# Attention probabilities brought to keys on partitions: 32x32 blocks transposed by VectorE and a trip through DRAM, in place of TensorE transposes and copies

## The chip, the cores and the metric

One core of one Trainium2 chip runs the whole kernel. The metric is the device time of one execution in microseconds (us). Before the change the median of three runs is 2646.62 us (2646.61 to 2647.22).

## The reference, cut to what matters

The input has 8 sequences of 512 tokens with 256 features. Each goes through four transformer layers (two layers, a recurrence with a learned matrix, then the same two layers again). The change lies in the local attention of these layers: 8 heads of 64, windows of 128 tokens; a query sees its own window and the one before, at most 128 keys back.

```
def _layer(x, wqkv, qs, ksc, wo, lg, lb, w1, b1, w2, b2):
    qkv = shift_token(x) @ wqkv                       # 256 -> 3 * 512
    q, k, v = heads of qkv;  q, k = rotary_xpos(l2norm(q) * qs, l2norm(k) * ksc)
    sim = einsum('bhwid,bhwjd->bhwij', 8 * q, k of this window and the one before)
    sim = where(mask, -max, sim)                      # mask: i < j, i > j + 128, no key
    attn = softmax(sim, axis=-1)
    out = einsum('bhwij,bhwjd->bhwid', attn, v)
    x = x + out @ wo
    ... layer norm, 256 -> 2 * 682, gated by gelu, 682 -> 256, added to x
```

All arithmetic is in float32.

## The kernel before, in words

**Work.** `sequence(b)` describes one sequence as a graph of nodes: two halves of two layers each, `attention` and `feed_forward`, with `ttt`, the recurrence, between the halves. An attention handles its four windows of 128 tokens one after another: transpose of x (`h.turn`), projections (`qk`, line 717, and `v`, line 804), rotation and norms, transposes of q and k (`qk.turn`, line 828). Then, twice per window, a group `g` of four heads:

- `sc` (line 868): TensorE computes scores. Its tile is used in quarters of 64 x 64, so that blocks that the window never reaches are left out. Queries lie on partitions, keys along the free dimension. From the second window on a query has 192 key columns (`nj`), in the first 128.
- `least` (line 911, DVE) adds the mask and finds the extreme of a row, `exp` (line 923, ACT) exponentiates and sums, one instruction per head; `recip` (line 936 DVE or 938 POOL) and `shares` (line 944, DVE or POOL) scale by the sum, one instruction of each for two heads.
- `pr.turn` (line 970): TensorE transposes the probabilities, 16 matmuls with the identity per group (8 in the first window), because the next product needs keys on partitions. `pr.copy` (line 629, in the helper `copy`, ACT or DVE) copies the two PSUM banks to `prT`.
- `po` (line 1007): TensorE multiplies values by the transposed probabilities, again in quarters; `po.copy` and `po.add` put the result together, and `py` (line 1058) projects it with `wo`. `x.attn` (line 1067) adds it to x.

There are 8 x 4 x 4 x 2 = 256 such groups. In the feed-forward, `hs.shift` (lines 1085, 1086, 1088) shifts x by one token with SBUF-to-SBUF DMAs; the matmuls are at lines 1151, 1242 and 1255.

**Order.** Nothing is ordered by hand. `Scheduler.run` goes through the graph like a planner: each node has an engine (or a choice of two), a cost in ns, buffers that it takes, and a `tail`, the ns until its result can be read. At each step the node that can start first goes next, corrected by `EARLY`, a table of ns per node name, and by `varied`, a pseudo-random correction by stretches of 5 us that the list `VARIED` steers. The instructions are then issued in that order on every engine, and each engine works through its own list in order. Up to three sequences are under way at a time (the pool `lane`). TensorE's nodes have a kind (`full`, `rows`, `quad`: the whole array, halves, quarters), and a change of kind has a planned cost.

**Queues.** All DMAs are issued by SyncE (SP), on one queue: loads of weights and x at the start, `hs.shift`, reloads of x (line 1760), and stores of the result (line 1790).

**Buffers** that the change touches: `pr` 6 of 128 x 512, two per group, with zeros at both edges of each row (written at line 1801), so that a transpose can read past the 192 columns; `prT` 2 of 128 x 1024; `s8` 8 for the sums; 8 PSUM banks, of which a group takes two for its transposes.

Of the kernel before, what the change touches and what calls it, by code (L numbers as in the profile page):

```python
# [12 lines left out]
ALU = mybir.AluOpType  # L13
# [12 lines left out]
GATE = 64  # L26
NH1 = 2 * NFC * P + GATE + REM
# [87 lines left out]
def t_pool(n, spread=False):  # L115
# [6 lines left out]
    "XT6": 200,  # L122
    "_full_quad": 850,
    "_full_rows": 350,
    "_quad_full": 400,
    "_quad_rows": 450,
    "_rows_full": 500,
    "_rows_quad": 650,
    "_table": -250,
    "base.x": -700,  # L130
    "base.y": 50,
    "base.z": -550,
    "below": -250,
    "block": 1000,
    "bx": 500,
    "bx.copy": -450,
    "bx6": 1000,
    "bx6.copy": -1000,
    "cross.mask": 2000,
    "down": -300,  # L140
# [4 lines left out]
    "gram": -50,  # L145
    "gram.copy": -750,
    "h.copy": -1650,
    "h.edge": 2100,
# [4 lines left out]
    "hs.rstd": -1350,  # L153
    "hs.stats": 100,
    "hs.zero": -400,
    "k.scale": 2350,
    "keys": -200,
    "keys.copy": -300,
    "kq": 5100,
    "kq.copy": -1000,  # L160
    "last": 200,
    "last.gelu": -650,
    "least": -250,
    "norm 0": 100,
    "norm 1": 400,
    "ones": 2100,
    "po": 3300,
    "po.add": 50,
    "po.copy": 100,
    "pr.copy": -250,  # L170
    "pr.turn": 150,
# [3 lines left out]
    "qk.add": -100,  # L175
    "qk.copy": 100,
# [3 lines left out]
    "qk.swapped": 2800,  # L180
    "qk.turn": 5050,
    "recip": 950,
    "remains": 650,
    "rest": -200,
    "rope": -2950,
    "sc": 2350,
    "sequence 4": 350,
    "shares": -50,
    "start": 1000,
    "tv": 2350,  # L190
    "u": 5500,
    "u.copy": -100,
    "v": -50,
    "value": 150,
    "w": 4650,
    "w.add": 350,
    "x.ffn": 200,
    "x.rstd": -1900,
    "x.scale": -500,
    "x.stats": 500,  # L200
    "xbx": 2650,
    "xbx.t": 500,
    "xbx6": 1000,
    "y": 300,
    "z.rstd": -400,
    "z.scale": 50,
    "z.stats": 5600,
    "zT": -450,
    "zero": -1000,
    "zn.rstd": -1850,  # L210
    "zn.scale": -350,
    "zn.stats": -500,
    "zn.turn": 4500,
# [6 lines left out]
    11539, 59206, 52431, 7169, 51312, 47193, 35081, 54701, 2496, 7793, 6049, 56177, 10364, 34536,  # L220
    8294, 4310, 20154, 19168, 52227, 29170, 16540, 21667, 50441, 20648, 28762, 21176, 51225, 49241,
    45956, 34971, 21009, 28142, 19477, 38168, 5557, 12352, 7023, 53196, 6017, 32604, 32616, 33833,
    43497, 35592, 8, 9511, 36946, 21011, 40384, 28542, 18616, 35469, 46717, 3648, 49052, 34713,
    26816, 29204, 8404, 4647, 15343, 36844, 570, 21424, 12355, 42492, 50428, 45178, 54350, 17920,
    13395, 135, 39989, 44533, 2549, 22957, 29261, 17027, 29544, 14357, 27402, 53285, 13020, 11910,
    26247, 40152, 22117, 30422, 46544, 22999, 49636, 47593, 30197, 3179, 35589, 32132, 42056, 18356,
    57054, 3385, 45135, 14935, 20770, 32612, 13353, 15733, 35692, 48376, 37702, 12678, 33060, 54960,
    27803, 54969, 53369, 31335, 34476, 36715, 13, 17472, 3933, 49344, 40320, 43761, 51808, 53819,
    30473, 58888, 28378, 53574, 53586, 34808, 30271, 11754, 5097, 46663, 4587, 12477, 2842, 20974,
    22949, 16164, 56345, 59752, 37818, 42810, 36514, 28003, 38920, 15614, 32190, 14889, 45329,  # L230
    56333, 3909, 22135, 44005, 49596, 54630, 11534, 50699, 55304, 13694, 14380, 32785, 48251, 51975,
    59596, 39815, 34672, 26684, 43342, 49501, 38504, 13035, 9055, 59153, 49831, 29616, 8451, 2950,
    5921, 10921, 22426, 31491, 10417, 40901, 35295, 21598, 37874, 47623, 56332, 58977, 50639, 51395,
    14345, 21523, 1611, 59581, 38356, 9024, 8797, 9600, 33490, 20077, 18908, 39770, 12624, 0, 51302,
    12996, 28627, 14230, 30261, 45539, 33994, 58844, 55888, 53070, 40769, 41472, 42381, 21824,
    25505, 26825, 37644, 26704, 31501, 49830, 52837, 21763, 24330, 27631, 47626, 31160, 32421,
    20990, 43125, 47451, 26149, 56263, 41669, 38285, 29128, 53275, 59120, 363, 15861, 23553, 38689,
    16, 59208, 8741, 59992, 24971, 2133, 29045, 13059, 56697, 49647, 42350, 46546, 32101, 980,
    58623, 42263, 42129, 58230, 58436, 55171, 53628, 11325, 17446, 17234, 26564, 12471, 44487,
    47246, 47905, 19512, 6228, 20309, 9884, 23474, 21539, 12749, 53397, 58236, 36711, 21477, 28615,  # L240
    11585, 23822, 4616, 960, 14012, 19245, 52408, 9606, 51939, 36194, 40143, 58969, 31327, 21363,
    19023, 20707, 24836, 4653, 46695, 9517, 40252, 20970, 35385, 8326, 20484, 11202, 51312, 9682,
    42952, 35195, 31373, 29093, 31724, 58081, 5082, 52637, 24194, 57630, 47639, 14785, 25712, 17698,
    27876, 35732, 43008, 43338, 18992, 8751, 5850, 25733, 15460, 31028, 26546, 27345, 36488, 44056,
    33295, 58977, 39749, 29184, 25121, 23756, 33811, 26536, 2260, 15160, 321, 39968, 25191, 31222,
    45604, 48604, 7672, 56893, 14684, 26720, 30312, 41919, 57072, 2421, 44875, 34765, 3604, 10279,
    45490, 35361, 22716, 21175, 46557, 5008, 49647, 1355, 7859, 39941, 43761, 4026, 49030, 9539,
    56965, 8358, 3988, 59899, 58021, 13265, 53954, 9411, 13889, 26300, 5547, 22515, 925, 22821,
    35389, 36309, 3233, 50482, 32683, 44192, 45433, 54698, 24152, 37273, 3714, 29516, 35158, 19134,
    31173, 30908, 46863, 51249, 42973, 41570, 7558, 58198, 43105, 36002, 53169, 27713, 15508, 57450,  # L250
    13353, 45327, 20959, 21312, 25608, 23768, 55045, 27334, 58634, 20168, 34664, 55665, 6316, 39132,
    11849, 10070, 18798, 46877, 11811, 49462, 58565, 1501, 28373, 7960, 55865, 56429, 52621, 1403,
    19983, 51522, 6552, 248, 6935, 6388, 4871, 4789, 20877, 23567, 24542, 21112, 42445, 40535,
    41468, 43567, 1697, 53106, 45256, 50440, 21162, 41824, 59524, 4758, 53095, 48105, 39745, 19805,
    15895, 4145, 51961, 47869, 41251, 39860, 1162, 32717, 5615, 59674, 43307, 49529, 2408, 1126,
    6903, 26424, 10998, 1128, 11983, 31727, 294, 20411, 37533, 25779, 45123, 39019, 22071, 17092,
    35693, 44717, 33182, 15800, 26669, 36844, 32178, 27395, 16355,
# [189 lines left out]
def macaron_kernel(ctx: ExitStack, tc: tile.TileContext, a: dict, out: bass.AP):  # L447
# [4 lines left out]
    ps = ctx.enter_context(tc.tile_pool(name="ps", bufs=1, space=bass.MemoryType.PSUM))  # L452
    engines = {"ACT": nc.scalar, "DVE": nc.vector, "POOL": nc.gpsimd}
# [15 lines left out]
    def both_of(*vals):  # L469
# [3 lines left out]

    pools = {
# [9 lines left out]
        "pr": buffers("pr", 6, [P, 8 * DH]),  # L484
        "prT": buffers("prT", 2, [P, 4, 4, DH]),
# [9 lines left out]
        "s8": buffers("s8", 8, [P, 8]),  # L495
# [23 lines left out]
    def load_x(b, w=None):  # L519

        if not w:
            lane[b], first_x[b] = Val("lane"), Val("x")
        own = slice(0, NW) if w is None else slice(w, w + 1)
        if w == 0 and b >= 2:
            taken[b] = node("lane.take", (b, -NW - 1), "SP", 0.0, lambda e: None, takes=[lane[b], first_x[b]], tail=0.0)
        order[0] += 1
        n = node(
            "load.x",
            (-1, order[0]) if b < 2 else (b, (w or 0) - NW),
            "SP",  # L530
            1500.0 if w is None else 450.0,
            lambda e: dma(first_x[b].ap[:, own, :], a["x"][b].rearrange("(w p) d -> p w d", p=P)[:, own, :]),
            [taken[b]] if b in taken else [],
            takes=[] if w or b in taken else [lane[b], first_x[b]],
            uses=[first_x[b]] if w or b in taken else [],
            tail=3600.0 if w is None else 2900.0,
        )
        L["x", b] = [n] * NW if w is None else [*L.get(("x", b), []), n]
# [8 lines left out]
    def load_layer(l):  # L547
# [38 lines left out]
        W[l] = (wqkv, rt, wo, lnp, w1, b1, w2)  # L586

# [18 lines left out]
    def sequence(b):  # L606
# [62 lines left out]
        def attention(x, l, ready):  # L669
# [3 lines left out]
            n_qk = n_v = n_k = None  # L673
            for w in range(NW):
# [6 lines left out]
                    [ready[w], L["ident"]],  # L681
# [3 lines left out]
                )  # L685
                n_h = copy(
# [174 lines left out]
                for g in range(2):  # L861

                    sc, prT = [Val("ps"), Val("ps")], Val("prT")
                    prs, sts = [Val("pr"), Val("pr")], [Val("s8"), Val("s8")]

                    def scores(sc=sc, g=g, w=w, qT=qT):
# [30 lines left out]
                        takes=[*sc, *prs, *sts],  # L897
# [3 lines left out]
                    n_w = []  # L901
                    for par in range(2):

                        st = sts[par]
                        pr = lambda k, n, par=par, prs=prs: prs[par].ap[:, DH + k * 3 * DH : DH + k * 3 * DH + n]
                        exps = []
                        for k in range(2):

# [33 lines left out]
                        def shares(e, st=st, par=par, prs=prs, nj=nj):  # L942
# [13 lines left out]
                                uses=[prs[par], st],  # L956
                                port=BOTH,
                            )
                        )


                    pts = [Val("ps"), Val("ps")]
# [909 lines left out]
```

## Time and profile before

| | |
|---|---|
| time, median of 3 runs | 2646.62 us |
| span of the profiled execution | 2645.8 us |
| granted TensorE clock, mean | 1.000 |
| busy: PE / DVE / ACT / POOL | 99% / 74% / 62% / 54% of the span |
| DMA | 44.69 MB moved, mean 17 GB/s |

The span runs from the first to the last instruction of one execution; the time has 0.8 us around it. PE is TensorE's matmuls, PEld its weight loads, which run beside matmuls; DVE is VectorE, ACT ScalarE, POOL GpSimd, SP SyncE. L970 is line 970 of the kernel. A group's line gives its busy time, the mean of one instruction in ns, and the idle time of the engine just before it with what ended that idle time.

### The profile page before, as it was taken

Reading aid. Unit: us, or ns where it says so; the run is one execution under the profiler, and the core shown is the slowest. Engines: PE = TensorE matmul, PEld = TensorE weight load, DVE = VectorE, ACT = ScalarE, POOL = GpSimd, SP = SyncE. Lnnn points to the kernel's source line nnn. Section 1 sums busy time; section 2 is a strip of 40 time slices with the busy share of each in tenths; the row PEclk is TensorE's granted clock in tenths of the full one; section 3 lists DMA queues with packets and bytes.
Section 4 is the critical chain, followed back from the end, with each engine's and each line's share of the span. In section 5 each row is a group of like instructions: output and inputs, shape, how many; then the busy total and the mean of one; then the engine's idle time right before and its main releaser. Section 6 shows DMA issues by size and latency. Waiting matters only on the chain.

```text
span 2645.8 us, 77025 instructions
## 1 busy us (share of the span) xinstructions
PE 2610.2 (99%) x30608; PEld 1961.5 (74%) x30608; DVE 1968.5 (74%) x5827; ACT 1647.9 (62%) x4328; POOL 1434.5 (54%) x2045
## 2 busy tenths in 40 slices
PE   8999999999999999999999999999999999999998
PEld 5777777677777777777777777777777777776776
DVE  7776776867878767877877678787677867867755
ACT  4666667655667756665566666667557665555754
POOL 8655464546565455654644466375445754546533
PEclk9999999999999999999999999999999999999999
DMA  5000000000100000000000001000001000000000
GB/s 186 10 8 10 17 8 16 6 8 8 34 7 10 9 11 28 8 10 7 19 23 9 8 10 30 6 10 9 7 8 32 11 8 10 22 7 6 14 9 17
DMA packets 59231, 44.69 MB, mean 17 GB/s; under 512 B 8140, under 2 KB 56440, under 8 KB 58872
## 3 DMA queue, kind: packets, MB, share of 16 engines
q1 hardware_dynamic: 58872, 39.77, 5.0%
q8 instruction: 241, 3.95, 0.6%
q14 instruction: 118, 0.97, 0.1%
HBM read 18.79 MB, written 4.19 MB: 9 GB/s over the span
## 4 chain that ended last, share of the span: by engine, by line
PE 66%; DVE 3%; ACT 2%; POOL 1%; issue 1%; DMA 0%; SPq 0%; DVEq 0%; ACTq 0%; POOLq 0%
PE ps L1151 16%; PE ps L717 12%; PE ps L1242 7%; PE ps L804 6%; PE ps L1058 6%; PE ps L1007 4%; PE ps L868 4%; PE ps L970 3%; PE ps L665 2%; PE ps L828 2%; PE ps L1255 1%; PE ps L1387 1%; PE ps L1498 1%; PE ps L1483 1%; ACT pr L923 0%
## 5 line engine op out<-in xcount | busy, mean ns | idle before, releaser
L1151 PE MATMUL ps<-h2T,w 128*128 128x256 f32 (+1 forms) x2816 | 651.5, 381 | 3.2 <-ACT h2T L1129 1.4
L1151 PEld LDWEIGHTS ps<-h2T,w 128*128 128x128 f32 (+1 forms) x2816 | 518.6, 188 | 121.9 <-issue 29.4
L717 PE MATMUL ps<-wqkv,hT 128*128 128x512 f32 x1024 | 487.5, 601 | 1.9 <-DMA wqkv<-in_wqkv_dram 1.8
L923 ACT ACTIVATE pr<-pr,s 128x192 f32<-128x192 f32 (+1 forms) x1024 | 439.8, 432 | 64.5 <-DVE s L911 61.2
L753 POOL TENSOR_TENSOR st<-st,powc 128x8 f32<-128x8 f32 x256 | 439.6, 1717 | 21.3
L911 DVE CUSTOM_DVE_ANT_0 pr<-ps,amask,st 128x192 f32<-128x192 f32 (+1 forms) x1024 | 353.8, 395 | 31.1 <-PE ps L868 28.1
L944 POOL TENSOR_TENSOR pr<-pr,s 128x384 f32<-128x384 f32 (+1 forms) x313 | 243.1, 787 | 202.4 <-DVE s L936 188.3
L717 PEld LDWEIGHTS ps<-wqkv,hT 128*128 128x128 f32 x1024 | 185.5, 191 | 160.1 <-issue 140.6
L1192 DVE SCALAR_TENSOR_TENSOR gT<-ps,b,gl 128x256 f32<-128x256 f32 x320 | 152.0, 482 | 195.5 <-PE ps L1151 167.1
L1242 PE MATMUL ps<-w,gT 128*128 128x256 f32 x1280 | 291.4, 380 | 0.0
L1242 PEld LDWEIGHTS ps<-w,gT 128*128 128x128 f32 x1280 | 241.5, 190 | 48.6 <-issue 16.3
L736 ACT ACTIVATE tmp<-ps 128x512 f32<-128x512 f32 x256 | 152.1, 596 | 195.8 <-DVE rot L761 134.6
L938 POOL TENSOR_TENSOR s<-s,powc 128x2 f32<-128x2 f32 x174 | 122.8, 707 | 278.7 <-ACT pr L923 276.1
L629 ACT COPY prT<-ps 128x512 f32<-128x512 f32 (+1 forms) x322 | 157.8, 542 | 151.1 <-PE ps L970 148.4
L1058 PE MATMUL ps<-wo,oT 128*128 128x256 f32 x1024 | 243.4, 380 | 0.5 <-DVE s L911 0.3
L804 PE MATMUL ps<-wqkv,hT 128*128 128x512 f32 x512 | 240.6, 594 | 0.1
L761 DVE TENSOR_TENSOR rot<-ps,rt 128x512 f32<-128x512 f32 x256 | 175.1, 686 | 74.4 <-PE ps L717 65.3
L1058 PEld LDWEIGHTS ps<-wo,oT 128*128 128x128 f32 x1024 | 191.2, 190 | 46.9 <-issue 16.1
L1173 ACT ACTIVATE gl<-ps,b 128x256 f32<-128x256 f32 x320 | 142.9, 474 | 108.4 <-PE ps L1151 100.2
L1007 PE MATMUL ps<-prT,v 64*64 64x128 f32 (+1 forms) x7168 | 198.1, 247 | 3.3 <-DVE prT L629 2.1
L868 PE MATMUL ps<-kT,qT 64*64 64x128 f32 (+1 forms) x7168 | 193.1, 250 | 4.2 <-issue 2.1
L923 ACT ACTIVATION_READ_ACCUMULATOR pr<-pr,s 128x1 f32 x1024 | 193.7, 189 | 0.0
(124 smaller groups left out, 4420.7 us busy)
## 6 DMA issues: line engine op xcount, KB each, us to landing
hs<-x SPq DMA_DIRECT2D x128, 64.0 KB
hs<-x SPq DMA_DIRECT2D x128, 63.5 KB
base<-in_x_dram SPq DMA_DIRECT2D x8, 512.0 KB
out_dram<-base SPq DMA_DIRECT2D x32, 128.0 KB
w<-in_w_dram SPq DMA_DIRECT2D x6, 640.0 KB
x<-in_x_dram SPq DMA_DIRECT2D x28, 128.0 KB
wqkv<-in_wqkv_dram SPq DMA_DIRECT2D x2, 1024.0 KB
hs<-x SPq DMA_DIRECT2D x96, 0.5 KB
```

Source lines behind the costliest of these rows:

```text
L717: nc.tensor.matmul(pp.ap, hT[w].ap[:, c * P : (c + 1) * P], wqkv[:, c, i * INNER : (i + 1) * INNER], start=(c == 0), stop=(c == 1),)
L753: nc.gpsimd.tensor_tensor(ss, ss, powc[:, 0:HEADS], ALU.pow)
L761: nc.vector.tensor_tensor(heads(rot.ap), heads(pp.ap), tab, ALU.mult)
L804: nc.tensor.matmul(pv.ap, hT[w].ap[:, c * P : (c + 1) * P], wqkv[:, c, 2 * INNER : 3 * INNER], start=(c == 0), stop=(c == 1),)
L868: nc.tensor.matmul(sc[par].ap[half(c), k * 4 * DH + at : k * 4 * DH + at + keys.stop - keys.start], qT.ap[half(par), 2 * g + k, half(c)], ...
L911: nc.vector.tensor_tensor_reduce(out=pr(k, nj), in0=sc.ap[:, k * 4 * DH : k * 4 * DH + nj], in1=amask[:, 0:nj] if w else amask[:, 3 * DH : ...
L923: nc.scalar.activation(pr(k, nj), pr(k, nj), AF.Exp, bias=st.ap[:, k : k + 1], scale=-1.0, accum_out=st.ap[:, 2 + k : 3 + k],)
L944: (nc.vector if e == "DVE" else nc.gpsimd).tensor_tensor(both, both, st.ap[:, 4:6].unsqueeze(2).to_broadcast([P, 2, nj]), ALU.mult)
L1007: nc.tensor.matmul(po[r].ap[half(par), k * P + first : k * P + first + cols * DH], v[j].ap[half(r), hd * DH : (hd + 1) * DH], prT.ap[half( ...
L1058: nc.tensor.matmul(py.ap[:, 0:D], oT.ap[:, c, :], wo[:, c, :], start=(c == 0), stop=(c == INNER // P - 1))
L1151: nc.tensor.matmul(dst.ap[0:rows, 0 : 2 * P], w1[:, kc, col : col + rows], h2T.ap[:, kc, :], start=(kc == 0), stop=(kc == 1),)
L1242: nc.tensor.matmul(py.ap[:, 0:D], gT.ap[:, at : at + P], w2[:, c, :], start=(c == 0), stop=False)
```

## The change: what it does

For a group's four heads the probabilities now lie in one buffer `pr` of 128 x 4 x 192, with one `recip` for four heads. In place of `pr.turn` and `pr.copy` stand three nodes:

- `pr.flip`: one DVE instruction transposes each 32 x 32 block of `pr` where it stands (24 blocks of 32 columns per row of blocks, 16 in the first window) into `flip`, with the four heads side by side.
- `pr.out`: four DMAs, one for each 32 queries, write `flip` to a DRAM tile `image` with keys as rows, in runs of 512 bytes. Queries 64 to 127 are written 64 rows lower, since their keys start 64 later.
- `pr.in`: one DMA reads 128 or 256 rows of the image back to `prT`, keys on partitions, 2048 bytes per row.

The parts of the image that nothing writes are set to zero once (`load_zeros`, two DMAs at the start, ahead of the second load of x). `weigh` (`po`) reads `prT` by its new layout; its matmuls are as many and as large as before. Buffers: `pr` 4, `flip` 3, `image` 6, `prT` 3, `s8` 5 with 16 columns. The DMA descriptor scratch is set to 1024. `h.turn` of a window now comes after that of the window before, and a sequence's lane is taken in order. The tables `EARLY` and `VARIED` have new values throughout, so the whole order of work is another one.

```
+    images = dram.tile([6, 2 * P, P // BLK, 4 * BLK], F32, name="images")
-        "pr": buffers("pr", 6, [P, 8 * DH]),
-        "prT": buffers("prT", 2, [P, 4, 4, DH]),
+        "pr": buffers("pr", 4, [P, 4, 3 * DH]),
+        "flip": buffers("flip", 3, [P, 3 * DH // BLK, 4, BLK]),
+        "image": [images[n] for n in range(images.shape[0])],
+        "prT": buffers("prT", 3, [P, 2, P // BLK, 4, BLK]),
...
+    def load_zeros():
+        flat = pools["flip"][0][0:DH].rearrange("p m h i -> p (m h i)")[:, 0 : 8 * BLK]
+        n = node("zeros", (-1, 0), "POOL", 400.0, lambda e: nc.gpsimd.memset(flat, 0.0))
+        def emit(e):
+            for lo, q in ((0, 2), (3 * DH, 0)):
+                dst = images[:, lo : lo + DH, q : q + 2, :].rearrange("n p q e -> p n (q e)")
+                dma(dst, flat.unsqueeze(1).to_broadcast(list(dst.shape)))
+        L["zeros"] = node("load", (-1, order[0]), "SP", 1000.0, emit, [n], tail=2500.0)
...
-                    def turn_pr(pts=pts, prs=prs, w=w):
-                        for h in range(4):
-                            for n in range(2 if w else 1):
-                                for r in range(2):
-                                    lo = DH + h % 2 * 3 * DH + (n * P - r * DH if w else 0)
-                                    at = (h * 2 + n if w else h) * DH
-                                    nc.tensor.transpose(
-                                        pts[r].ap[:, at : at + DH],
-                                        prs[h // 2].ap[half(r), lo : lo + P],
-                                        ident[half(r), half(r)],
-                                    )
-                    n = pe("pr.turn", 4 * T_TURN * (2 if w else 1), turn_pr, n_w, takes=[*pts, prT], uses=prs, kind="rows")
-                    n_t = 2 if w else 1
-                    tps = [copy("pr.copy", n_t * 4 * DH, ...) for r in range(2)]
+                    nb = nj // BLK
+                    def flip(prs=prs, turn=turn, nb=nb):
+                        nc.vector.transpose(
+                            turn.ap[:, 0:nb], prs.ap[:, :, 0 : nb * BLK].rearrange("p h (m i) -> p m h i", i=BLK)
+                        )
+                    n = dve("pr.flip", 60.0 + 1.045 * 4 * nj, flip, n_w, takes=[turn], uses=[prs])
+                    def out_of(e, turn=turn, image=image, nb=nb, w=w):
+                        for q in range(P // BLK):
+                            lo = q // 2 * DH if w else P
+                            rows = image.ap[lo : lo + nb * BLK, q, :].rearrange("(m k) e -> k m e", k=BLK)
+                            dma(rows, turn.ap[q * BLK : (q + 1) * BLK, 0:nb].rearrange("k m h i -> k m (h i)"))
+                    n = node("pr.out", prio(), "SP", 2120.0, out_of, [n], takes=[image], uses=[turn], tail=1750.0)
+                    def into(e, prT=prT, image=image, w=w):
+                        if w:
+                            dma(prT.ap.rearrange("p n q h i -> p n (q h i)"),
+                                image.ap.rearrange("(n p) q e -> p n (q e)", n=2))
+                        else:
+                            dma(prT.ap[:, 1].rearrange("p q h i -> p (q h i)"),
+                                image.ap[P : 2 * P].rearrange("p q e -> p (q e)"))
+                    tps = [node("pr.in", prio(), "SP", 540.0, into, [n, L["zeros"]], takes=[prT], uses=[image], tail=1800.0)]
```

## The prediction

> **What bounds the kernel now.** I read the page's first two parts, then the groups by line, the waits, the chain in one stretch, a timeline, and the DMA views.
>
> The page:
>
> ```profile
> PE 2610.2 (99%) x30608; PEld 1961.5 (74%) x30608; DVE 1968.5 (74%) x5827; ACT 1647.9 (62%) x4328; POOL 1434.5 (54%) x2045
> ...
> PE   8999999999999999999999999999999999999998
> ...
> PEclk9999999999999999999999999999999999999999
> ```
>
> TensorE is busy in every slice at full granted clock, so the kernel's length is the length of TensorE's list of work; 35.6 us of the span of 2645.8 are idle there. The other engines have a quarter or more to spare. The groups that the change touches (busy us, mean ns of one, idle before):
>
> ```profile
> L970 PE MATMUL ps<-sq,pr 64*128 64x64 f32 x3584 | 144.1, 225 | 3.1 <-DVE pr L944 0.7 <-POOL pr L944 0.7 <-DVE tmp L767 0.7
> L629 ACT COPY prT<-ps 128x512 f32<-128x512 f32 (+1 forms) x322 | 157.8, 542 | 151.1 <-PE ps L970 148.4
> L629 DVE COPY prT<-ps 128x512 f32<-128x512 f32 (+1 forms) x190 | 112.4, 622 | 52.3 <-PE ps L970 51.3
> ```
>
> From the waits, what TensorE itself loses to these copies (us in total, times, longest):
>
> ```profile
> PEld ps L1007 <- ACT prT L629: 7.8, 18, 1.0
> ```
>
> So the transposes count in full, the copies next to nothing. Busy time overstates the transposes, since neighbours overlap. The chain of waits between 1300 and 1312 us (start, us) gives their place on the path:
>
> ```profile
> 1301.74 1.14 PE ps L970 x32
> 1302.88 0.50 PE ps L828 x16
> ```
>
> and the timeline has the same block start at 1301.67 and the next one's weights at 1302.66: 0.99 us for 32.
>
> **What is removed.** All 3584 transposes go. At 0.99 us per 32 that is 112 x 0.99 = 111 us, at 1.14 it is 128 us. The bounds are 103 us (28.8 ns each, a least-squares fit of block starts in the trace, so without the changes of array tiling around a block) and 147 us (busy 144.1 plus 3.1 idle). The built programs' order shows that changes between the three tilings of TensorE (whole array, half, quarter) fall only from 556 to 525, so most boundaries stay. I take **120 us**. Nothing else in TensorE's list changes: every other matmul has its old count. 1 us of memsets goes on POOL, hidden.
>
> Also removed are 512 copies (157.8 us of ACT, 112.4 of DVE), half of the reciprocals, and by the order 40 table loads of ACT at 1283 ns (51 us). All lie beside TensorE: worth nothing at the end, but room.
>
> **What is added on VectorE.** 192 block transposes of 128x768 and 64 of 128x512. No row shows one. The nearest are elementwise f32 rows: 128x384 at about 0.55 us and 128x512 at 0.71 us, so some 1.2 ns an element: 1.0 us for 768 and 0.7 us for 512, together 192 x 1.0 + 64 x 0.7 = 237 us; bounds half (118) and double (474). I take 237, the rate of the nearest rows. The order also gives DVE fewer reciprocals (338 to 225), shares (199 to 150) and adds (157 to 118), some 72 us less. DVE: 1968 - 112 - 72 + 237 = 2021 us, with the bounds 1902 to 2258, against some 2525 on TensorE: it stays below, so the transposes cost latency only. ACT falls to about 1440, POOL (more shares and adds, fewer powers) stays near 1435.
>
> [...]
>
> **What is added on SyncE and the DMA engines.** Per group (four heads of one window, 256 in all) four stores of 32 partitions in 512 B runs and one load of up to 512 KB: 1024 + 256 issues. At 0.505 us (the row below) that is some 650 us on a queue that now issues for about 260. The bytes, 92 MB out and 117 MB in, are 83 GB/s over the span; the trace moved 377 GB/s at a share of 1.08, so a quarter of capacity. In volume this is hidden. In time it is not: the wait of SP for the landed stores sits in the same in-order queue as the loads of x and the shift of hs.
>
> ```profile
> L1085 SPq DMA_DIRECT2D hs<-x x128: 495/505/862, 43.0 to 2611.5; - x128
> ...
> L1086 SPq DMA_DIRECT2D hs<-x x128: 597/619/684, 43.6 to 2612.3; - x128
> ```
>
> The round trip: the first load of x (128 KB) is issued at 0.73 us and its reader starts at 2.93, 2.2 us. So the stores take 3 x 0.5 + 2.2 = 3.7 us, the load 2.2 + 384 KB at 377 GB/s (1.0) = 3.2 us, with the block transpose **7.9 us**. From below: stores at 0.35 us per issue (the row of the result's store, L1790) and 1.7 us from the last issue to its last semaphore event in the trace (the shortest of L1790), 2.8 us, the load 2.6 us: 6.4 us.
>
> [...]
>
> **What it replaces, and what is late next.** I paired each group's instructions in the trace by order. From the end of scores (L868) to the start of weighting (L1007) pass 16.1 us in the median; of these 8.4 us until shares (L944) end and 6.6 after them (tenth 3.1, quarter 4.4, three quarters 10.8), in which transposing and copying need 1.85. So 4.8 us are spare. The changed program's order puts TensorE work of 17.6 us between scores and weighting where the old one, counted alike, has 16.4; in the shortest tenth 14.4 against 11.7. With shares where they were, 7.8 us are open for 7.9 us of work: the spare is used up at the median, and the tightest tenth is some 2 us late. Between, the list was drawn up with the new steps in it (863 + 3870 + 2340 ns and hops, 7.1 us), so a weighting should be late only by what the real trip takes beyond that, 0.8 us. One stall also delays the scores behind it, so it counts about once per 17.6 us: 2525/17.6 = 143 stretches x 0.8 us x half of them tight = 57 us; from below 0 (a trip of 6.4), from above 143 x 0.85 = 122. I take **45 us**, a little under the middle.
>
> Sum against the profiled execution: 2645.8 - 120 + 45 = 2570.8, and with the 0.8 us between span and median time **2572 us** (-2.8%).
>
> **The rivals.**
>
> *All hidden.* The trip takes 7.1 us or less and waits are as rare as now: 2646.6 - 120, at most 15 us better from fewer PSUM banks held (two per group go), 2512 to 2540, say **2527**. For it: the 4.8 us of spare above, 3 buffers of prT where 2 were. Against it: shares to weighting needs four times the latency with 1.2 us more cover. Chance 0.25.
>
> *The gain is mostly eaten* (waits of 75 to 115 us): 2602 to 2641, say **2620**. Chance 0.15.
>
> *Slower: the shift of hs blocks the trip.* L1086 moves 127 partitions, and the windows after its issue at 43.63 show (last columns DMA share, GB/s):
>
> ```profile
> 45.00:46.00 1.00, 1.00 (x38) 0.93 (x36) 1.00 (x2) 1.00 (x3) 1.00 (x2) 1.00 0.08 23
> 46.00:47.00 1.00, 1.00 (x49) 0.94 (x43) 0.48 (x2) 1.00 (x3) 0.92 (x2) 1.00 0.10 21
> 47.00:48.00 1.00, 1.00 (x46) 0.89 (x45) 0.60 (x2) 0.32 (x2) 1.00 (x2) 1.00 0.07 22
> ```
>
> One engine of sixteen works for over four us. A store or load behind it that spreads over all engines has a sixteenth of its bytes in that line. In the new order of SP 76 of the 128 shifts are followed directly by a store of probabilities and 32 by a load. If each of these 108 comes within the 4 us and loses 3 us with 1 us spare, that is 216 us: 2646.6 - 120 + 216 = 2743; it decides from 1.1 us lost per shift on (120/108). Against it: most of these stores have to wait for their block transpose anyway, and a pair of groups has 20 us. I price the case at **2690**. Chance 0.15.
>
> *The change doesn't do what it says* is ruled out: the built program has no L970. *VectorE as the bound* needs its transposes at over 740 us, triple my value; I leave it inside the slower case.
>
> **How the numbers follow.** Forecast 0.43 (2540 to 2602); all hidden 0.25; mostly eaten 0.15, with 0.02 of it inside 0.2% of no change; slower 0.15; 0.02 for a time below 2512. The range of 8 in 10 runs from 2515 to 2660: it leaves out 0.03 below and some 0.12 above. 0.2% is 5 us, what a measurement of this kernel can tell from no change. Faster 0.43 + 0.25 + 0.13 + 0.02 = 0.83, same 0.02, slower 0.15.
>
> **What would show it.** TensorE's busy time 110 to 147 us lower with no matmul of the identity on pr; its idle time, 35.6 us now, up by some 45, put down to DMA prT ahead of the weighting. If that idle time is under 20 us more, the hidden case holds; if it stands right after shifts of hs, the slower mechanism is at work whatever its size. DVE at 1.9 to 2.26 ms busy, a block transpose at about 1 us. From the last exp of a group to its weighting 3 us or more longer than now. Wrong altogether would be a granted clock below 1.00, or DVE busy above 95%.

## The result, and the profile after

The changed kernel takes **2813.64 us** (median of four runs, 2793.94 to 2814.94), the kernel before 2646.61 us (2645.74 to 2647.22). The ratio is 1.0616, 95% interval 1.0585 to 1.0648: 6% slower, outside the range and on the side to which the prediction gave 0.15.

The page of the changed kernel: busy time by engine, TensorE's slices and its granted clock, the DMA queue that SP fills, and the two groups that matter (busy us, mean ns of one, idle before).

```profile
PE 2594.1 (92%) x27024; PEld 1918.6 (68%) x27024; DVE 2012.6 (72%) x5666; ACT 1461.8 (52%) x3991; POOL 1427.1 (51%) x1980
...
PE   7998999999999899999989999988999999998997
...
PEclk9999999999999899999999999999999999999998
...
q1 hardware_dynamic: 317720, 250.35, 34.0%
...
L1018 PE MATMUL ps<-prT,v 64*64 64x128 f32 (+1 forms) x7168 | 228.0, 266 | 177.7 <-DMA prT<-images 169.9
...
L984 DVE STREAM_TRANSPOSE flip<-pr 128x768 f32<-128x768 f32 (+1 forms) x256 | 231.4, 905 | 11.8 <-POOL pr L965 5.7
```

Two things are to be seen. TensorE has 3584 instructions fewer, and is busy for only 16 us less (2594.1 against 2610.2), while its idle time has gone from 35.6 to 219.0 us (span 2813.1). And the idle time has one name. The waits (us in total, times, longest):

```profile
PE ps L1018 <- DMA prT<-images: 169.9, 96, 5.5
...
PEld ps L1018 <- DMA prT<-images: 78.9, 49, 6.0
```

The weighting (L1018) waits for the load that brings `prT` in from DRAM. The second row belongs to the weight loads and covers much of the same time (65.8 of its 78.9 us), so the two are not added up. The next wait of PE itself is 6.2 us in all.

Why did the busy time hardly fall? The mean granted clock is 0.964, where it was 1.000; the row of digits hides it, since a slice is 70 us long. TensorE's timeline at one of the waits (start and length in us, in brackets the idle time ahead and its releaser):

```profile
406.85 0.72 PE L849 MATMUL ps<-sq,rot 64*128 64x64 f32 x16
409.93 0.90 PE L1018 MATMUL ps<-prT,v 64*64 64x128 f32 x32 [2.36 <-DMA prT<-images]
```

SP's timeline of the same place:

```profile
400.95 4.84 SPq L994 DMA_DIRECT2D images<-flip  x8
405.96 2.04 SPq L1000 DMA_DIRECT2D prT<-images  x2
```

and four windows of 3.4 us around it (window, length, busy time of PE, PEld, DVE, ACT, POOL with counts, granted clock, DMA share, GB/s):

```profile
404.20:407.60 3.40, 3.37 (x42) 2.42 (x40) 2.30 (x5) 1.18 (x3) 3.32 (x4) 1.00 0.55 114
407.60:411.00 3.40, 1.07 (x53) 1.10 (x55) 0.00 (x0) 1.35 (x4) 3.24 (x4) 1.00 0.83 269
411.00:414.40 3.40, 3.40 (x88) 3.40 (x84) 2.86 (x13) 0.54 (x2) 0.93 (x2) 0.50 0.65 180
414.40:417.80 3.40, 3.40 (x62) 2.03 (x55) 2.23 (x12) 3.27 (x15) 0.23 (x1) 1.00 0.13 43
```

The eight stores and two loads of two groups stand one behind the other on SP. The first load is issued at 405.96; TensorE has nothing to do from 407.57 on and starts the weighting at 409.93, 3.97 us after the issue. The wait costs 2.36 us. Then, from 411.00 to 414.40, the granted clock is 0.50. **The wait is paid a second time**, at half clock, in work that counts as busy. Over the whole trace the clock stands at half for 202.6 us in 43 episodes of 3.4 to 6.8 us (4.5 us in all before the change). Ahead of each lies a stretch of 3.4 us in which TensorE was idle for 1.3 to 3.4 us, mostly 2 to 2.5, in one piece or in several. In the clock records of the trace all episodes begin on one grid with steps of 3.41 us, so the other steps can be counted too. Of those with the clock at full, none of 703 with under 1.2 us of idle time was followed by half clock, 10 of 27 with 1.2 to 2.0 us were, and 32 of 34 with more; the two exceptions lie in the first 12 us of the kernel. (The last episode, at the kernel's end, is not in this count.)

From the semaphore events of the trace come the steps of the trip, from the start of an issue to the last landing: the block transpose of 128x768 0.97 us, four stores 3.50 us from the first issue, the load of 512 KB 4.22 us (shortest 3.42), the load of 256 KB 2.82 us. Together 0.97 + 3.50 + 4.22 = 8.7 us, where the list that orders the work counts 863 + 3870 + 2340 ns = 7.1. These are the medians of the steps alone. With each group's transpose, stores and load paired in order, a load of 512 KB lands 10.3 us after the start of its transpose in the median, since SP often has other DMAs to issue first: the load is issued 0.6 us after the stores have landed, in a quarter of the groups 2.0 us or more. The list plans SP's queue too, so this is not all an error of the list; but the 7.9 us of the prediction have no term for it.

**The theory after the result:** the trip is about 1.6 us longer than the list believes, all of it in the load (1.9 us over its 2.34; the stores take 0.4 less than planned); TensorE comes to the weighting too early, waits, and each wait of some 2 us also halves its clock for a while. The rivals: the shift of `hs` with its 127 partitions holds the queue up (the prediction's slower case); the traffic or the block transposes slow everything down by themselves; or the new order of work is a worse one for reasons that have nothing to do with the trip.

### The profile page after: what moved, and what is told of

Read it like the earlier page. It is cut to its first block, busy times and chain, and to the rows that moved or that the text cites. A ratio compares the mean times of both kernels' runs of the same rounds, so it can differ in the third digit from the quotient of the medians.

```text
span 2813.1 us, 71036 instructions
## 1 busy us (share of the span) xinstructions
PE 2594.1 (92%) x27024; PEld 1918.6 (68%) x27024; DVE 2012.6 (72%) x5666; ACT 1461.8 (52%) x3991; POOL 1427.1 (51%) x1980
## 5 line engine op out<-in xcount | busy, mean ns | idle before, releaser
L965 POOL TENSOR_TENSOR pr<-pr,s 128x384 f32<-128x384 f32 (+1 forms) x362 | 284.0, 801 | 510.3 <-DVE s L955 507.5
L738 PE MATMUL ps<-wqkv,hT 128*128 128x512 f32 x1024 | 491.9, 606 | 3.7 <-DMA wqkv<-in_wqkv_dram 2.1
L774 POOL TENSOR_TENSOR st<-st,powc 128x8 f32<-128x8 f32 x256 | 432.1, 1688 | 21.3
L1018 PE MATMUL ps<-prT,v 64*64 64x128 f32 (+1 forms) x7168 | 228.0, 266 | 177.7 <-DMA prT<-images 169.9
L1018 PEld LDWEIGHTS ps<-prT,v 64*64 64x64 f32 x7168 | 199.1, 146 | 208.8 <-DMA prT<-images 78.9
L1062 DVE TENSOR_TENSOR oT<-oT,ps 128x256 f32<-128x256 f32 (+1 forms) x256 | 97.9, 385 | 219.2 <-ACT oT L649 201.6
L649 ACT COPY oT<-ps 128x256 f32<-128x256 f32 x232 | 86.3, 372 | 321.2 <-PE ps L1018 319.8
L825 PE MATMUL ps<-wqkv,hT 128*128 128x512 f32 x512 | 244.1, 601 | 0.1
L984 DVE STREAM_TRANSPOSE flip<-pr 128x768 f32<-128x768 f32 (+1 forms) x256 | 231.4, 905 | 11.8 <-POOL pr L965 5.7
L889 PE MATMUL ps<-kT,qT 64*64 64x128 f32 (+1 forms) x7168 | 218.5, 274 | 3.4 <-ACT qT L649 1.7
L658 POOL TENSOR_SCALAR st<-st 128x1 f32<-128x1 f32 (+1 forms) x192 | 49.9, 260 | 328.5 <-DVE st L1110 232.1
```

What stands on the lines that cost most here:

```text
L738: nc.tensor.matmul(pp.ap, hT[w].ap[:, c * P : (c + 1) * P], wqkv[:, c, i * INNER : (i + 1) * INNER], start=(c == 0), stop=(c == 1),)
L774: nc.gpsimd.tensor_tensor(ss, ss, powc[:, 0:HEADS], ALU.pow)
L825: nc.tensor.matmul(pv.ap, hT[w].ap[:, c * P : (c + 1) * P], wqkv[:, c, 2 * INNER : 3 * INNER], start=(c == 0), stop=(c == 1),)
L889: nc.tensor.matmul(sc[par].ap[half(c), k * 4 * DH + at : k * 4 * DH + at + keys.stop - keys.start], qT.ap[half(par), 2 * g + k, half(c)], ...
L965: (nc.vector if e == "DVE" else nc.gpsimd).tensor_tensor(both, both, st.ap[:, 8 + 2 * k : 10 + 2 * k].unsqueeze(2).to_broadcast([P, 2, nj] ...
L984: nc.vector.transpose(turn.ap[:, 0:nb], prs.ap[:, :, 0 : nb * BLK].rearrange("p h (m i) -> p m h i", i=BLK))
```

## The experiments

### a_no_turn: the removal alone

The kernel before without transposes and copies, in its own order; nothing is put in their place.

```
-                        for h in range(4):
+                        for h in range(0):
...
-                                prT.ap[half(r), h, n : n + cols, :],
+                                still[half(r), h, n : n + cols, :],      # still = wo rearranged
```

> The kernel before, every instruction in its old order, but the 3584 transposes of probabilities and the 512 copies of them are not issued; weighting reads a tile of weights in their place, so the product of probabilities and values is left out of the result in substance, and the size of every other instruction is as before. It measures the term of the prediction that was removed, by itself. If the transposes are worth what the prediction took (120 us, bounds 103 to 147), the time is 2527 us (2500 to 2544). If they were hidden in pipelining and worth little (under 60 us), the time is over 2587, and the changed kernel's loss is that much smaller to explain.

Measured: 2588.99 us (2587.13 to 2590.03), ratio 0.9783 (0.9769 to 0.9798).

```profile
PE 2511.3 (97%) x27024; PEld 1854.4 (72%) x27024; DVE 1861.0 (72%) x5637; ACT 1503.4 (58%) x4006; POOL 1434.2 (55%) x2045
```

TensorE's busy time falls by 98.9 us, a little less than the lower bound of 103, and the time only by 57.6: idle time rises from 35.6 to 74.0 us. The order was drawn up with the transposes in it, and other waits grow, such as this one, which was 1.0 us before:

```profile
PE ps L868 <- ACT qT L629: 14.0, 18, 1.2
```

What the transposes took, they also hid in part. The removal is worth 58 us in this order; whether an order without these new waits would keep the 99 was not tried.

### b_still: everything kept, but nobody waits

The changed kernel with all its block transposes, stores and loads; only the weighting reads a tile of weights that never changes in place of `prT`.

```
-                                prT.ap[half(r), n // 2, q : q + 2 * cols, h, :],
+                                still[half(r), n // 2, q : q + 2 * cols, h, :],      # still = wo rearranged
```

> The changed kernel with all its block transposes, stores and loads in their old order, but weighting reads a tile of weights, so that TensorE never waits for the trip through DRAM (and the load no longer waits for the buffer's last reader); the weighted values are wrong in substance, the matmuls are as many and as large. Theory 1, the trip is longer than the list of work allows for, and TensorE waits for it and then runs at half clock: both go, 2510 to 2545 us, granted clock 0.99 or more, idle time of TensorE under 60 us. Theory 2, the DMA traffic (209 MB) or the block transposes slow the engines or make DVE late, whoever waits: the time stays above 2650. Theory 3, the new order is bad in itself, with the rest of the list late as well: 2600 to 2750.

Measured: 2570.91 us (2568.93 to 2577.62), ratio 0.972 (0.9705 to 0.9735).

```profile
PE 2503.8 (98%) x27024; PEld 1848.4 (72%) x27024; DVE 2008.9 (78%) x5666; ACT 1458.7 (57%) x3991; POOL 1426.9 (56%) x1980
```

The whole loss is gone with the wait, and 76 us are won on the kernel before. The traffic is all there (loads still take 4.24 us, DVE is as busy as in the changed kernel) and the order is the same, so none of them makes the kernel slow by itself, without the wait. The trace also shows how early the order places the weightings. From the start of a group's block transpose to its weighting pass 9.3 us in the median (groups with the 512 KB load), while the load lands after 10.3: of the 190 such weightings whose load's landing can be read, 116 begin before it, by 1.9 us in the median. The time lies somewhat above the 2510 to 2545 expected, because 63.3 us of idle time stay here too. This run divides the loss: against it the changed kernel has 155.7 us more idle time (219.0 - 63.3) and 90.3 us more busy time in the same matmuls (2594.1 - 2503.8). With the 78.7 us that this run's span lies below that of before: 2645.8 - 78.7 + 155.7 + 90.3 = 2813.1. The 90.3 us agree with the clock records: the changed kernel has 202.6 us at half clock and this run 19.6, and half of the difference is 91.5.

### d_spread: the shift over more DMA engines

The changed kernel with the shift of 127 partitions cut into moves of 112 and 15.

```
-                    dma(hs.ap[1:P, w, P:D], x.ap[0 : P - 1, w, P:D])
+                    for lo, hi in ((1, 113), (113, P)):
+                        dma(hs.ap[lo:hi, w, P:D], x.ap[lo - 1 : hi - 1, w, P:D])
```

> [...] One more issue of about 0.5 us per shift. Theory of the prediction's slower rival, the one-engine move holds up the stores and loads behind it: up to 216 us come back, 2600 to 2720 us. Theory 1, the trip is too long even when nothing is ahead of it (load of 512 KB 4.1 us in the median with no shift in flight, 4.8 with one; one load in five has a shift in flight): at most 40 us come back, 2770 to 2815.

Measured: 2765.87 us (2762.16 to 2769.91), ratio 1.0457 (1.044 to 1.0475). 48 us come back. The DMA issues of this run (KB each, median us from issue to landing):

```profile
prT<-images SPq DMA_DIRECT2D x192, 512.0 KB, 4.0
images<-flip SPq DMA_DIRECT2D x768, 96.0 KB, 2.0
images<-flip SPq DMA_DIRECT2D x256, 64.0 KB, 1.8
...
hs<-x SPq DMA_DIRECT2D x128, 64.0 KB, 1.9
hs<-x SPq DMA_DIRECT2D x128, 56.0 KB, 2.0
```

The shift lands in 2.0 us, where it took 5.0 (by its semaphore events in the changed kernel). At the 21 to 23 GB/s of the prediction's windows the 56 KB of its longer move would take 2.5 to 2.7 us, so more than one engine seems to carry them; that is an estimate from these numbers, and how many do was not shown. But the loads still take 4.0 us and the weighting still waits 96 times for them:

```profile
PE ps L1018 <- DMA prT<-images: 141.4, 96, 5.3
```

The rival is real and small: 48 us over the 108 shifts that a store or load follows by the prediction's count are 0.44 us each, where it needed 1.1 to decide. (In the changed kernel's trace 71 shifts have a store directly behind them and 32 a load; with these 103 it is 0.46.) It is also a little more than my theory allowed (40 at most).

### e_fill: useless work against the half clock

The changed kernel with 140 needless matmuls of 128x512 (two records each in the trace), placed ahead of the 68 weightings that had waited longest. If waits cost only their own length, this can gain nothing.

```
+                        for _ in range(FILL.get(order[1], 0)):
+                            nc.tensor.matmul(po[0].ap, wo[:, 0, 0:P], wqkv[:, 0, 0:INNER], start=True, stop=True)
+                        order[1] += 1
```

> The changed kernel with 140 matmuls more (128x512, two passes of 427 ns each, 120 us in all) that compute nothing of use, placed ahead of the 68 weightings for which TensorE waited 1 us or more in the changed kernel's trace, as many as fit into each wait; they write the bank that the weighting then overwrites. Nothing is left out. Theory: the half clock (202 us of the changed kernel's span) follows from TensorE being idle for more than half of a stretch of 3.4 us; with the waits filled the clock stays up, most of its 90 us come back, 2720 to 2770 us, granted clock over 0.985, though TensorE has more work. Rival: the clock falls for another cause (the DMA traffic, the kind of work), or the matmuls only add to the list: 2800 to 2900 us, clock as before.

Measured: 2753.11 us (2751.9 to 2758.82), ratio 1.0403 (1.0386 to 1.0421): **60 us faster than the changed kernel, with more work in it.**

```profile
PE 2651.8 (96%) x27304; PEld 1901.4 (69%) x27304; DVE 2009.9 (73%) x5666; ACT 1460.1 (53%) x3991; POOL 1426.1 (52%) x1980
```

The group of the added matmuls:

```profile
L1016 PE MATMUL ps<-wqkv,wo 128*128 128x512 f32 x280 | 140.1, 625 | 0.6 <-ACT oT L650 0.6
```

The mean clock is 0.997, with 18 us at half in place of 202.6. The fill adds 140.1 us of busy time, takes 113.8 from the idle time, and the rest of TensorE's work takes 82.4 us less (2594.1 - 2511.7): 140.1 - 113.8 - 82.4 = -56 us of span. The 82.4 us come near the 90.3 of b_still. The DMA traffic is the same and the matmuls are more, and the clock rises: idle time of TensorE lowers it here, not its work or the traffic.

### h_half: a shorter load

The changed kernel with a load of 256 KB for every group; the weighting reads its one half of `prT` twice.

```
-                        if w:
-                            dma(
-                                prT.ap.rearrange("p n q h i -> p n (q h i)"),
...
+                        dma(
+                            prT.ap[:, 1].rearrange("p q h i -> p (q h i)"),
...
-                                prT.ap[half(r), n // 2, q : q + 2 * cols, h, :],
+                                prT.ap[half(r), 1, q : q + 2 * cols, h, :],
```

> The changed kernel, but every load brings 256 KB (one half of the keys) in place of 512 KB, and weighting reads that half for both, so keys of the window before are left out of the result in substance; matmuls, stores and order are as before. In the changed kernel the 256 KB loads land 2.8 us after the start of their issue and the 512 KB loads 4.2 us. Theory 1, the length of the trip beyond what the list allows decides: 1.4 us less for three groups in four give back more than half of the 243 us that a kernel without waits gains, 2640 to 2700 us, granted clock over 0.985. Rival, one more or less long wait is as good as another (the shift's one-engine move, or stores that are late): under 60 us, 2750 to 2800.

Measured: 2692.19 us (2682.82 to 2693.66), ratio 1.0167 (1.0149 to 1.0185). Its busy times:

```profile
PE 2546.0 (95%) x27024; PEld 1879.5 (70%) x27024; DVE 2009.2 (75%) x5666; ACT 1460.6 (54%) x3991; POOL 1426.4 (53%) x1980
```

The load takes 2.78 us, 1.4 less, and 121 us come back, half of the 243 that lie between the changed kernel and b_still: 75.6 us of idle time and 48.1 of busy time. The clock is 0.982, a little under the 0.985 expected. So the length of the load carries half of the loss, and waiting and clock shrink together. Medians don't explain the rest: a trip of 7.3 us is only 0.2 over the list's, and 80 us of idle time above b_still remain. The spread does in part: of the 116 weightings that are early in b_still, 76 are so by more than the 1.4 us saved here, and 56 waits for the load are left in this run. In the changed kernel's trace a load behind a shift takes 4.8 us and a load behind another 4.6, against 3.9 for the others; which of these make up the rest was not tried.

### p_true and p_true2: the list told the truth

If the cause is that the list places weightings too early, true lengths should mend it. Both are the whole change with the spread shift and measured lengths in the list that orders the work; `EARLY` and `VARIED` were searched anew against that list, for p_true2 further.

```
-                    n = dve("pr.flip", 60.0 + 1.045 * 4 * nj, ...)
+                    n = dve("pr.flip", 160.0 + 1.06 * 4 * nj, ...)
-                    n = node("pr.out", prio(), "SP", 2120.0, ..., tail=1750.0)
+                    n = node("pr.out", prio(), "SP", 2000.0, ..., tail=1700.0)
-                    tps = [node("pr.in", prio(), "SP", 540.0, ..., tail=1800.0)]
+                    tps = [node("pr.in", prio(), "SP", 450.0, ..., tail=4050.0 if w else 2850.0)]
-                moved.append(node("hs.shift", prio(), "SP", 500.0, ..., tail=5120.0))
+                moved.append(node("hs.shift", prio(), "SP", 2650.0 if w < NW - 1 else 2100.0, ..., tail=1800.0))
```

> The changed kernel whole, with the shift in two moves, and with the lengths that the changed kernel's runs showed told to the list of work: stores 2.0 us of issue and 1.7 us until landed, load 0.45 and 4.05 us (2.85 in the first window), shift 2.65 us of issue and 1.8, block transposes 0.97 us. EARLY and VARIED were searched anew for these lengths, so the order is another one on every engine. Theory 1, the change loses because the list expected the load's rows 1.9 us too early: hardly a wait for prT is left (under 40 us), granted clock over 0.99, 2585 to 2635 us, which is less than the kernel before. Rival, the trip can't be hidden with these buffers (its length and not the plan's error decides): waits of 100 us or more remain and the time is over 2680.

Measured: 2624.88 us (2621.06 to 2628.37), ratio 0.9916 (0.9899 to 0.9932). The weighting waits 15.0 us for its load.

> As p_true, with a further search of EARLY and VARIED for the same lengths of the trip. If the list of work is now a fair picture of the chip, a list that is 6 us shorter gives 2612 to 2626 us, granted clock 0.99 or more. If what is left is lost to things that the list does not know, no gain: 2622 to 2640.

Measured: **2607.71 us** (2606.05 to 2611.17), ratio 0.9857 (0.984 to 0.9873), better than expected. Its page:

```profile
PE 2536.8 (97%) x27024; PEld 1843.5 (71%) x27024; DVE 1992.8 (76%) x5630; ACT 1499.5 (58%) x4018; POOL 1451.1 (56%) x2019
...
PEclk9999999999999999999999999999999999999999
...
L1021 PE MATMUL ps<-prT,v 64*64 64x128 f32 (+1 forms) x7168 | 198.1, 248 | 24.8 <-DMA prT<-images 20.7
```

The weighting now waits 20.7 us for its load, where it waited 169.9, idle time is 69.0 us and the clock 0.999. The loads are hardly shorter (3.97 us in the median, against 4.22, and 4.04 in d_spread); they are expected. The new order leaves 12.6 us in the median from the start of the block transpose to the weighting, where b_still, with the old order, has 9.3. These runs change the lengths and the search together; a new search with the old lengths was not run, so the share of each is not known. Against b_still 38.7 us are left, 33.0 of them busy time. TensorE's tiling changes 699 times in this order, 525 times in the changed kernel's; that these changes make up the difference was not tried.

### q_before: the control

The kernel before with the spread shift, and its order searched anew in the same way. Transposes and copies are kept.

> The control: the kernel before, with the shift in two moves and EARLY and VARIED searched anew in the same way and for longer than in the run p_true, to see whether the gain of p_true over the kernel before is one of the search and of the shift alone. If it is, this kernel is as fast as p_true, 2600 to 2635 us. If the change itself is worth something once its trip is planned, this one stays at or above the kernel before: 2640 to 2700 us, with TensorE's waits spread over many lines.

Measured: 2657.71 us (2657.43 to 2658.26), ratio 1.0044 (1.0029 to 1.0059). Its TensorE is as full as before:

```profile
PE 2620.4 (99%) x30608; PEld 1958.8 (74%) x30608; DVE 1950.2 (73%) x5828; ACT 1637.3 (62%) x4354; POOL 1410.5 (53%) x1996
```

Search and spread give the kernel before nothing; this order is 11 us slower than its own old one. That control searched for longer than p_true, so the 0.8% of p_true is hardly a gain of the search or of the shift alone; it is put down to the change, once the order knows its cost. The 1.4% of p_true2 rest on a further search, and whether the control's search equals that one is not on record.

## Why the prediction was wrong

| step | predicted | measured |
|---|---|---|
| transposes removed, TensorE's busy time | 120 (103 to 147) us | 99 us (a_no_turn), 106 (b_still) |
| the same, net of waits that come up | not priced | 58 us (a_no_turn), 76 (b_still) |
| block transposes on DVE: in all; one of 128x768 | 237 us; 1.0 us | 231.4 us; 0.97 us |
| DVE, ACT, POOL busy | 2021, 1440, 1435 us | 2012.6, 1461.8, 1427.1 us |
| four stores | 3.7 us | 3.50 us |
| load | 3.2 us | 4.22 us (512 KB), 2.82 (256 KB) |
| whole trip over the list's 7.1 us | 0.8 us | 1.6 us |
| waits of the weighting | 45 (0 to 122) us | 156 us (idle time over b_still's) |
| clock | 1.00 | 0.964, 90 us |

**The bound was right.** TensorE's list set the end before and sets it after, now with its waits; VectorE has 28% to spare, ACT and POOL lost or kept their time as reckoned, the DMA engines are at 34% (I said a quarter).

**The step that failed is what is late next:** "a weighting should be late only by what the real trip takes beyond that, 0.8 us", and 45 us for it all. It took the lateness of a weighting from the excess of the trip alone. Two sizes in it were wrong. First, the load. I took the 2.2 us of one small load of x and added the bytes at 377 GB/s, the best rate of the trace. The two sizes measured here give 256 KB in 4.22 - 2.82 = 1.40 us, 187 GB/s, half of that rate. Second, the number of late weightings: with the real excess my own formula gives 143 x 1.6 x 0.5 = 114 us, and 156 came (the waits show 96 of 1.8 us in the mean). "Half of them tight" was a guess without a row behind it, and the 45 us lie below the 57 of the formula, also without a reason. In b_still, where nothing waits, 116 of 190 weightings come too early, by 1.9 us in the median and up to 5.6: the room that the order leaves and the trip both vary from group to group, with SP's queue and with loads of 3.9 to 4.8 us by what is in flight, and that makes waits that an excess of medians doesn't show.

**What was missing altogether is the clock.** The prediction named a clock below 1.00 as what would make it wrong, and had no price for it. It made 90 us, and it follows the waits (b_still, e_fill): 156 us of waiting cost 246, so each microsecond waited costs 1.6 here. Without it, the time would have come to some 2813 - 90 = 2723, an estimate from these two terms: still slower. The waits alone would have decided the sign, and the clock made 3% into 6%.

**The removal** was worth less than its lower bound in a_no_turn, and a part of it came back as waits of other steps, so "the transposes count in full" did not hold.

**The slower rival** had the right sign for the wrong reason: the blocked queue is there, at 48 of the 216 us reckoned in full. *All hidden* (2527) fell by the same load; an order that counts on a slow trip hides nearly all of it (p_true2, 2607.7), and even with no wait for the load at all (b_still) the time is 2571.

## What to carry to other kernels

Where an order of work is drawn up ahead from a list of durations, a change that replaces a short step by a trip through DMA is worth what the list knows of the trip (here 2813.6 us with 2.34 us for the load in the list, 2607.7 with 4.50, the shift in two moves and a new search): measure its landing times in place, at its own size and with its neighbours in flight (here 4.22 us where 3.2 were predicted, and 3.9 to 4.8 by what was in flight), before judging the change by its time. Price a wait of TensorE at more than its length when it lasts about 2 us (here each microsecond waited cost 1.6), and look at the mean granted clock first when busy time doesn't fall with the instructions (here 0.964, with 3584 instructions fewer and 16 us less of busy time). An experiment in which the reader looks at something that is already there (b_still) tells in one run what waiting costs and what everything else costs.

## What the runs showed of the hardware

- Idle time of about 2 us within 3.4 us was enough for half clock. In the changed kernel the clock fell 43 times, for 3.4 or up to 6.8 us, 202.6 us in all. Over the changed kernel and the seven runs a_no_turn to p_true2, steps of 3.41 us at full clock with under 1.2 us of idle time were never followed by half clock (0 of 5897); with 1.2 to 2.0 us 33 of 116 were, with more 77 of 93, and the 16 exceptions lie in the first 12 us of a kernel. The wait of 2.36 us shown above was followed by half clock.
- Filling 68 of the waits with needless matmuls gained 60 us (e_fill).
- A move of 127 partitions landed in 5.0 us (changed kernel); as 112 and 15 it landed in 2.0, and the kernel ran 48 us faster (d_spread).
- A store of 96 KB from 32 partitions landed in 2.0 us after the start of its issue (d_spread); at the 22 GB/s of the prediction's windows, in which one engine works, its bytes alone would take 4.5, an estimate. In the changed kernel's trace the DMA share was 0.69 with stores alone under way (33.9 to 34.8 us) and 0.96 with loads alone (67.9 to 69.2 us); one engine of sixteen would be 0.06.
- A block transpose of 128x768 f32 on VectorE took 0.97 us, one of 128x512 0.71 us in the median (changed kernel).
